# A four-layer network with expert layers on one core: expert slots in a room per expert, layer 3's routing during its attention, second biases inside the expert groups

## The chip, the cores and the metric

The kernel runs on one core of a Trainium2 chip. The core has a matrix engine (TensorE, PE in the profile; PEld is its loading of weights), a vector engine (VectorE, DVE), a scalar engine (ScalarE, ACT), a general engine (GpSimd, POOL) and a queue engine (SyncE, SP)[...] and 16 DMA engines. On-chip memory has 128 partitions; matrix products land in PSUM. The metric is the device time of one execution in microseconds. All figures below are the core's own.

## The reference

Input x is 32 sequences of 256 tokens with 128 channels (8192 tokens). Four layers follow, each x = x + attn(norm(x)) and then x = x + ffn(norm(x)), in float32. What matters here:

```
# layer 0 ffn: expert-choice experts and a shared expert
# layer 1 ffn: 8 experts, hidden 512, top 2 of 8 by x @ gate_w + gate_b
gw = softmax(top_w)
out = sum_e combine[:, e] * (gelu(x @ w1[e] + b1[e]) @ w2[e] + b2[e])
shared = gelu(x @ ws1 + bs1) @ ws2 + bs2
# layer 3 ffn, on its normed input x:
x = layernorm(x + mha(x, 16 heads), ln1_g, ln1_b)
gp = softmax(x @ w_group + b_group)        # 4 groups, the best is taken
ep = softmax(x @ w_expert + b_expert)      # 2 experts in it, the best is taken
y_e = relu(x @ w1[e] + b1[e]) @ w2[e] + b2[e]   # hidden 256
x = layernorm(x + g_prob * e_prob * y_e, ln2_g, ln2_b)
```

The layer-3 result is added to that layer's input. The biases b2 and the norms' gains and shifts are not zero or one in the inputs.

## The kernel before

x stays on chip as 64 tiles of 128 tokens (K.x, named x_sb in the profile). Eight stage functions run one after the other: l0_attn, l0_ffn, l1_attn, l1_ffn, l2_attn, l2_ffn, l3_attn, l3_ffn. A scheduler orders instructions on each engine, except where manual_schedule says that an engine keeps the written order (the expert groups and the attention, on PE, ACT and DVE). Memory of a finished pool is given to the next tiles; the first instruction that writes the new tile then waits for the last use of the old.

*Expert slots (class Slots).* In layers 1 and 3 each token's row of 130 numbers (128 channels, the row number where its result goes, its weight) is sent to a table in the chip's main memory, sorted by expert. fill writes blank rows early in the kernel (POOL, 56 DMAs for both tables, behind layer 0's attention). places works out every token's slot: products with triangular and all-ones matrices count how many earlier tokens chose the same expert, a scan over tiles sums them, each expert's rows are rounded up to groups of 256, and so an expert's first slot is known only once all tokens are routed. send_all writes the tokens with indirect DMAs from POOL, one per tile and rank (line 382; 128 in layer 1, 64 in layer 3). experts then takes groups of 256 rows: DVE copies the group's expert weights (w, line 418, from w_all at an offset read from group_of), SP loads the rows (xs, line 420), PE transposes them, multiplies twice (hp line 436, o line 452) with ACT's activation between, DVE scales by the weight (y, line 457) and POOL scatters the result with two indirect DMAs (f_back, line 388). Fetch, rise and fall of three neighbouring groups overlap. There are 72 groups in layer 1 and 40 in layer 3; blank rows fill the rest. join loads the results in order and adds them.

*Layer 1 ffn.* Norm, gate (lp, line 1309), choice of two experts (beat, top), places, sends. While POOL sends, PE works the shared expert in 16 blocks of 512 tokens (lines 1346 to 1359), and the second biases, combine times b2, in 16 further blocks (lines 1363 to 1372, through the PSUM tiles hp and o that the shared expert uses).

*Layer 3 ffn.* attention (line 1389) is also used by layer 2. It goes through 32 batches (one sequence each) in steps: PAIRS = 8 steps t to a batch, and in each step a written mixture of scores for a later batch (s and top), weights and values for the present one (t, e, o), and in certain of the eight places p = t % 8 the projection of a batch ahead and the output of the one before (heads, back, join). rows(b) makes the normed input of a batch on POOL (line 1893). Its PSUM tile m (pool pm) is shared by projections and outputs. Before the first batch its tiles val, k and q are cleared on POOL (lines 1417 to 1423). After attention come the first norm (DVE, line 121, then gain and shift on POOL, lines 1936 and 1937), transposes and gate (ge, line 1966), softmax and argmax over groups and experts, places, 64 sends, bias blocks (line 2003), experts, join, and the second norm with the last addition. The weights w_all are loaded in a burst on SP just after attention (lines 1922 and 1923). build then stores the result in eight DMAs.

## Time and profile before

| | us |
|---|---|
| three runs | 3464.90, 3453.68, 3464.75 (median 3464.75) |
| the profiled execution | 3465.69 |
| its span | 3463.6 |
| mean granted clock of PE | 0.874 |
| PE busy | 2774.8 (80%) |
| DVE busy | 1871.7 (54%) |
| ACT busy | 1331.2 (38%) |
| POOL busy | 801.7 (23%) |

The stages, as read from the trace (us from the span's start): l0_attn to 367, l0_ffn to 874, l1_attn to 1014, l1_ffn to 1631 (norm and routing to 1108, sends to 1277, bias blocks to 1320, experts to 1598, join), l2_attn to 2261, l2_ffn to 2393, l3_attn to 2490, l3_ffn to the end (attention to 3070, first norm and routing to 3158, sends to 3241, experts to 3369, join to 3386, second norm and stores).

In the views, a time is that of one profiled execution. "idle before <-releaser" says how long an engine stood before an instruction and what ended the wait. A busy PE is not PE at its peak, and a DMA-issuing instruction is not counted as busy. Groups are named by line of the kernel, engine, operation and the program's tile names.

### The profile page before, as it was taken

The numbers are of one execution on the slowest core, as the hardware profiler recorded it, in microseconds if no ns is written. First come the engines' busy times: TensorE is split into PE (matmuls) and PEld (weight loads), VectorE is DVE, ScalarE is ACT, GpSimd is POOL, SyncE is SP. The second block draws the span as 40 slices with busy tenths as digits, with TensorE's granted clock in tenths as the row PEclk, the third lists the DMA queues.
The fourth block names the chain that finished last, engine by engine and source line by source line (L and its number), as shares of the span: only waits on it lengthen the run. The fifth ranks groups of instructions, "written<-read, shape, count | busy, mean of one in ns | idle before, by whom it ended". The sixth has DMA issues, their size and how long they took to land.

```text
span 3463.6 us, 57988 instructions
## 1 busy us (share of the span) xinstructions
PE 2774.8 (80%) x22018; PEld 1924.6 (56%) x22018; DVE 1871.7 (54%) x4141; ACT 1331.2 (38%) x2801; POOL 801.7 (23%) x1009
## 2 busy tenths in 40 slices
PE   5999787999979829994699999967888888975660
PEld 4765444448557518993466666656455555554550
DVE  6115345337674003445666666555677777774338
ACT  3323432224623303441155555611256666631120
POOL 0001420000232753554200000002140000035664
PEclk9899799999987958997599999958889999975695
DMA  2386420010010111224344444200144444410232
GB/s 64 122 256 202 131 69 1 29 31 3 2 55 9 51 46 46 72 71 127 98 125 125 125 125 125 77 3 6 35 139 124 125 125 128 121 29 27 69 101 74
DMA packets 252694, 285.05 MB, mean 82 GB/s; under 512 B 31971, under 2 KB 228192, under 8 KB 244224
## 3 DMA queue, kind: packets, MB, share of 16 engines
q1 hardware_dynamic: 213632, 228.32, 22.9%
q0 software_dynamic: 17984, 42.53, 3.8%
q10 hardware_dynamic: 20800, 10.49, 1.2%
q8 instruction: 175, 2.87, 0.3%
q14 instruction: 103, 0.84, 0.1%
HBM read 156.69 MB, written 122.45 MB: 81 GB/s over the span
## 4 chain that ended last, share of the span: by engine, by line
PE 55%; DVE 14%; POOL 6%; issue 5%; DMA 5%; ACT 4%; SPq 0%; POOLq 0%; ACTq 0%; DVEq 0%
PE t L1595 7%; PE o L1615 6%; PE hp L436 4%; PE o L452 4%; POOL f_rows L382 3%; PE s L1540 3%; PE m L1627 2%; DVE top L1553 2%; PE m L1500 2%; DMA f_rows<-row,slot 2%; POOL f_back L388 2%; DVE y L121 2%; PE o L1144 2%; ACT e L1603 2%; PE g L1105 2%
## 5 line engine op out<-in xcount | busy, mean ns | idle before, releaser
L1553 DVE TENSOR_REDUCE top<-s 128x6 f32<-128x768 f32 (+1 forms) x512 | 556.2, 1089 | 255.7 <-PE t L1476 88.9
L1603 ACT ACTIVATE e<-t 128x384 f32<-128x384 f32 (+1 forms) x1024 | 508.9, 546 | 177.8 <-PE t L1476 104.9
L1595 PE MATMUL t<-q,k 64*128 64x256 f32 (+1 forms) x2048 | 420.0, 306 | 38.1 <-ACT e L1603 37.1
L1540 PE MATMUL s<-k,q 48*128 48x256 f32 (+1 forms) x2048 | 421.0, 329 | 4.4 <-DVE top L1553 3.7
L1595 PEld LDWEIGHTS t<-q,k 64*128 64x128 f32 x2048 | 293.7, 189 | 155.9 <-ACT e L1603 91.8
L1615 PE MATMUL o<-e,val 128*32 128x256 f32 (+1 forms) x4096 | 303.1, 368 | 0.1
L1540 PEld LDWEIGHTS s<-k,q 48*128 48x128 f32 x2048 | 293.5, 196 | 11.5 <-DVE top L1553 8.0
L388 POOL DMA_INDIRECT f_back<-y,place x224 | 219.4, 980 | 184.6 <-DVE y L457 138.4
L442 ACT ACTIVATE h<-hp,w 128x256 f32<-128x256 f32 x368 | 154.3, 470 | 254.7 <-PE hp L436 249.1
L436 PE MATMUL hp<-xT,w 128*128 128x256 f32 x736 | 186.5, 393 | 24.4 <-DVE xT L427 24.3
L452 PE MATMUL o<-w,h 128*128 128x128 f32 x1472 | 184.8, 277 | 0.0
L452 PEld LDWEIGHTS o<-w,h 128*128 128x128 f32 x1472 | 175.6, 194 | 0.1
L1735 POOL TENSOR_SCALAR xn<-x_sb,mean_a,r_a 128x128 f32<-128x128 f32 x64 | 58.9, 929 | 459.6 <-PE m L1489 446.7
L436 PEld LDWEIGHTS hp<-xT,w 128*128 128x128 f32 x736 | 134.6, 195 | 44.4 <-DVE xT L427 30.0
L1476 PE MATMUL s<-hideq,pick 64*128 64x128 bf16 x1024 | 146.1, 230 | 0.0
L1476 PE MATMUL t<-hidek,pick 64*128 64x128 bf16 x1024 | 145.8, 225 | 0.0
L418 DVE COPY w<-w_all 128x1028 f32 (+1 forms) x112 | 67.5, 602 | 131.4 <-DMA f_rows<-row,slot 90.5
L128 PE MATMUL t<-ident,xn 128*128 128x128 f32 x320 | 72.0, 353 | 79.7 <-DVE xn L121 63.7
L382 POOL DMA_INDIRECT f_rows<-row,slot x128 | 122.8, 959 | 40.4 <-issue 29.9
L689 PE MATMUL up<-wc,hT 128*128 128x128 f32 x768 | 131.8, 313 | 0.0
L1494 POOL TENSOR_TENSOR y<-y,bias 128x256 f32<-128x256 f32 x32 | 22.0, 688 | 441.7 <-PE m L1489 441.7
L1615 PEld LDWEIGHTS o<-e,val 128*32 128x32 f32 x4096 | 81.2, 108 | 63.3 <-ACT out L1621 5.9
(522 smaller groups left out, 5493.8 us busy)
## 6 DMA issues: line engine op xcount, KB each, us to landing
d<-half SPq DMA_DIRECT2D x256, 256.0 KB
tz<-kpad SPq DMA_DIRECT2D x64, 512.0 KB
q<-d SPq DMA_DIRECT2D x128, 256.0 KB
k<-d SPq DMA_DIRECT2D x128, 256.0 KB
f_rows<-blank POOLq DMA_DIRECT2D x56, 260.0 KB, 3.2
xs<-f_rows SPq DMA_DIRECT2D x112, 130.0 KB
y_d<-ys SPq DMA_DIRECT2D x32, 256.0 KB
yt<-y_d SPq DMA_DIRECT2D x32, 256.0 KB
```

Of the source, the lines that this page charges most:

```text
L382: i = self.K.nc.gpsimd.indirect_dma_start(self.rows, bass.IndirectOffsetOnAxis(ap=slot[:, j : j + 1], axis=0), row, None)
L388: i = self.K.nc.gpsimd.indirect_dma_start(self.back, bass.IndirectOffsetOnAxis(ap=place, axis=0), row, None)
L436: nc.tensor.matmul(hp[:, i, :], w[:, (c + i) * P : (c + i + 1) * P], xT, start=True, stop=True,)
L442: nc.scalar.activation(h[:, c + i, :], hp[:, i, :], act, bias=w[:, b1 : b1 + 1])
L452: nc.tensor.matmul(o[:, i, :], h[:, c, i * P : (i + 1) * P], w[:, F + c * D : F + c * D + D], start=c == 0, stop=c == FC - 1,)
L689: nc.tensor.matmul(o, hT[:, 2 * blk + b, s : s + P], wc[:, j, cs], start=j == 0, stop=False)
L1476: nc.tensor.matmul(t.rearrange("p (n q) -> p n q", n=3)[:, 0:3:2, 64 * n : 64 * n + 64], pick[r, n, :], hide[name][r], start=False, stop=n ...
L1540: nc.tensor.matmul(s[:, j, lo:hi], q[r, p, h * P : (h + 1) * P], k[r, p, 0 : hi - lo], start=h == 0, stop=not causal and h == 1,)
L1553: nc.vector.tensor_reduce(tops[b][:, :, :, p].rearrange("q h j -> q j h"), out_of["s"][:, :, 0:used].rearrange("q j (h k) -> q j h k", h=n ...
L1595: nc.tensor.matmul(t[:, kh * SEQ : kh * SEQ + SEQ - late], k[r, p, kh * P : (kh + 1) * P], q[r, p, late:SEQ], start=kh == 0, stop=not caus ...
L1603: nc.scalar.activation(e, t, AF.Exp)
L1615: nc.tensor.matmul(o[32 * i : 32 * i + 32, late:SEQ], val[b % RING][:, kh, 4 * g + i, :], exps[4 * g + i][:, kh * SEQ : kh * SEQ + SEQ - l ...
```

## The change

1. The table of slots gets a fixed room for each of the 8 experts, 8448 rows each, so a slot no longer depends on the other experts' totals. The tables grow from 18432 and 10240 rows to 67584 each, and fill writes them in DMAs of 6 rows per partition that lie together in memory (176 DMAs instead of 56).
2. places is a generator that takes a chunk of tiles and carries the counts on in seen. finish computes from the totals which expert a group belongs to and at which row it starts; experts reads the start into a register of SP for its load. SP joins the engines in written order there.
3. In layer 3, the first norm, the routing and the sends run as steps (route) of attention's loop, for the chunks of tiles 0-16, 16-32, 32-48, 48-56 and 56-64, each once its tiles are complete: two steps in each attention step, and a step that needs PE only in two places of eight. What is left over runs after the last attention step. The norm is applied by ACT, gain and shift by POOL. Argmax over the groups is taken first and only the two experts of the best group are compared. The second norm's shift is added to x on POOL during attention. The tiles of begin, the norm's parameters and gate weights are taken ahead of attention; w_all is loaded in a pool opened after it.
4. The second biases are split into three bf16 parts and added inside each group by a product of depth 3 with a row of ones; the 16 bias blocks of each of the two layers are gone. In layer 1's shared expert one product per block adds its bias, and the output products accumulate onto it. w is 128 columns wider, of which three rows hold the parts.
5. The end goes in quarters of 16 tiles: results loaded on SP and added, statistics, norm on ACT, gain and addition on DVE, a store per four tiles. Layer 1's join loads on SP alone.

```diff
+    def second_biases(self, pool, dst, name):
+
+        nc = self.nc
+        n = dst.shape[1]
+        src = self.ins[name].rearrange("n d -> (n d)").unsqueeze(0)
+        t = pool.tile([3, n * D], F32, name="rows3")
+        nc.sync.dma_start(t, src.partition_broadcast(3))
+        rows = self.split(pool, t, self.parts(pool, 3), name)
+        nc.vector.tensor_copy(dst, rows.rearrange("p (n d) -> p n d", n=n))
...
     def close(self, lo, hi):
+        for _ in self.steps(lo, hi):
+            pass
+
+    def steps(self, lo, hi):
...
         nc.vector.tensor_add(mean, st[:, :, 1], st[:, :, 4])
+        yield
...
+    ROOM = NT * P + GROUP
...
-        self.count = self.groups * self.GROUP
+        self.count = self.NE * self.ROOM
...
-        n = 4
+        n = 6
...
-        rows = self.rows.rearrange("(t p) w -> p t w", p=P)
+        rows = self.rows.rearrange("(c p n) w -> c p n w", p=P, n=n)
...
+            nc.gpsimd.dma_start(rows[i], t)
...
+    def begin(self, pool, most):
+
+        nc = self.K.nc
+        self.every = pool.tile([P, P], BF16, name="every")
+        self.first = pool.tile([P, P], BF16, name="first")
+        nc.gpsimd.memset(self.every, 1.0)
...
+        self.go_on = pool.tile([P, self.NE, most], F32, name="go_on")
+        nc.gpsimd.memset(self.go_on, 1.0)
+        nc.gpsimd.memset(self.go_on[:, :, 0:1], 0.0)
+        self.seen = pool.tile([P, self.NE], F32, name="seen")
+        self.floor = pool.tile([P, self.NE], F32, name="floor")
+        for t in (self.seen, self.floor):
+            nc.gpsimd.iota(
+                t, pattern=[[self.ROOM, self.NE]], base=0, channel_multiplier=0,
+                allow_small_or_imprecise_dtypes=True,
+            )
...
+    def places(self, pool, bank, picks, out):
+
+
+        NE = self.NE
...
+        t = bank()
...
+        yield "PE"
+        nc.tensor.matmul(before, self.first, taken, start=True, stop=True)
+        nc.tensor.matmul(total, self.every, taken, start=True, stop=True)
...
+        slot = new("slot").rearrange("p (e n) -> p e n", e=NE)
+        nc.vector.tensor_sub(slot, sums, total)
+        nc.vector.tensor_add(slot, slot, before)
+        yield
+        nc.vector.tensor_add(slot, slot, self.seen.unsqueeze(2).to_broadcast([P, NE, n]))
+        nc.vector.tensor_add(self.seen, self.seen, sums[:, :, n - 1])
+        yield
+        for m, u in zip(picks, out):
+            mine = new("mine").rearrange("p (n e) -> p n e", e=NE)
+            s = pool.tile([P, most], F32, name="place")[:, 0:n]
+            nc.vector.tensor_mul(mine, m, slot.rearrange("p e n -> p n e"))
+            yield
...
+    def finish(self, pool, long, expert, start):
...
+                at = nc.sync.value_load(
+                    start[0:1, g : g + 1], min_val=0, max_val=self.count - self.GROUP
+                )
+                xs = gp.tile([P, N, self.WIDE], F32, name="xs")
+                nc.sync.dma_start(
+                    xs, self.rows[bass.ds(at, self.GROUP)].rearrange("(n p) w -> p n w", p=P)
+                )
                 at = nc.vector.value_load(
-                    group_of[0:1, g : g + 1], min_val=0, max_val=(self.NE - 1) * LONG
+                    expert[0:1, g : g + 1], min_val=0, max_val=(self.NE - 1) * LONG
                 )
...
+                b2 = gp.tile([3, D], BF16, name="b2")
+                nc.scalar.copy(b2, w[0:3, 2 * F + FC :])
...
+                    nc.tensor.matmul(o[:, i, :], self.every[0:3, :], b2, start=False, stop=True)
...
-                engines={nc.tensor.engine, nc.scalar.engine, nc.vector.engine}
+                engines={nc.tensor.engine, nc.scalar.engine, nc.vector.engine, nc.sync.engine}
...
+        nc.gpsimd.memset(w_all[:, :, 2 * F + FC :], 0.0)
...
+        S.begin(sp, NT)
...
+                K.second_biases(K.pool(bs, "f1b", 1), w_all[0:3, :, 2 * F + FC :], "f1_b2")
...
+            S.finish(cp, LONG, expert, start)
+            for n in range(2):
+                S.belongs(row, 0, NT, n)
+                nc.gpsimd.tensor_copy(row[:, :, D + 1], weight[:, n, :])
+                for j in range(NT):
+                    S.send(slots[n][:, j : j + 1], row[:, j, :])
...
+                nc.tensor.matmul(
+                    o, S.every[0:3, :], b2.unsqueeze(1).to_broadcast([3, 4, D]), start=True,
+                    stop=False,
+                )
...
-            for blk in range(NBLK):
-                t = ph.tile([NE + 1, 512], F32, name="hp")
-                for i in range(4):
-                    nc.tensor.transpose(t[:, i * P : (i + 1) * P], cmb[:, 4 * blk + i, :], K.ident)
-                cmbT = hw.tile([NE + 1, 512], F32, name="cmbT")
-                nc.scalar.copy(cmbT, t)
-                o = po.tile([P, 4, D], F32, name="o")
-                for i in range(4):
-                    nc.tensor.matmul(
-                        o[:, i, :], cmbT[:, i * P : (i + 1) * P], b2, start=True, stop=True
-                    )
-                xb = K.x[:, 4 * blk : 4 * blk + 4, :]
-                nc.vector.tensor_add(xb, xb, o)
             cs.close()
 
...
+        if more:
+            more(t, bank)
+
+    def bank():
+        return pm.tile([P, 512], F32, name="m")
...
-        for t in range(-LEAD, total + PAIRS):
+        for t in range(-LEAD, total + PAIRS + (PAIRS if more else 0)):
...
+        S.begin(sp, 16)
+        ln = K.load_bcast(sp, "f3_ln", 4 * D).rearrange("p (n d) -> p n d", n=4)
...
+                K.second_biases(K.pool(bs, "f3b2", 1), b2, "f3_b2")
...
+            def route(bank, lo, hi):
+
+
+                n = hi - lo
+                for _ in after.steps(lo, hi):
+                    yield
...
+                for k in range(lo, hi, 4):
+                    four = y[:, k : k + 4, :]
+                    for j in range(k, k + 4):
+                        nc.scalar.activation(
+                            y[:, j, :], y[:, j, :], AF.Identity, bias=nmr[:, j : j + 1],
+                            scale=after.r[:, j : j + 1],
+                        )
+                        yield
+                    nc.gpsimd.tensor_mul(four, four, spread(4, 0))
+                    nc.gpsimd.tensor_add(four, four, spread(4, 1))
+                for k in range(lo, hi, 4):
+                    yield "PE"
+                    t = bank()
+                    K.transpose4(t, y[:, k : k + 4, :])
+                    yT = rw.tile([P, 512], F32, name="yT")
+                    nc.scalar.copy(yT, t)
+                    yield "PE"
+                    t = bank()[:, 0 : 4 * (NG + NE)].rearrange("p (n e) -> p n e", n=4)
+                    for i in range(4):
+                        nc.tensor.matmul(
+                            t[:, i, :], yT[:, i * P : (i + 1) * P], gate_w, start=True, stop=True
+                        )
+                    nc.vector.tensor_add(
+                        lge[:, k - lo : k - lo + 4, :], t,
+                        gate_b.unsqueeze(1).to_broadcast([P, 4, NG + NE]),
+                    )
+                yield
...
+                yield from S.places(rw, bank, [pick.rearrange("p n g e -> p n (g e)")], [slot])
+                for j in range(lo, hi):
+                    S.send(slot[:, j - lo : j - lo + 1], row[:, j, :])
+            work, held = [], [None]
+            cuts = [16, 32, 48, 56, 64]
+            def more(t, bank):
+                if t is None:
+                    while work:
+                        if next(work[0], work) is work:
+                            work.pop(0)
+                    return
+                b, p = t // PAIRS - 2, t % PAIRS
+                if p == 0 and 0 <= b < NB:
+                    after.take(y, 2 * b, 2 * b + 2)
+                    two = K.x[:, 2 * b : 2 * b + 2, :]
+                    nc.gpsimd.tensor_add(two, two, spread(2, 3))
+                    if 2 * b + 2 in cuts:
+                        i = cuts.index(2 * b + 2)
+                        work.append(route(bank, cuts[i - 1] if i else 0, cuts[i]))
+                for _ in range(2):
+                    if work:
+                        if held[0] == "PE" and p not in (1, 2):
+                            return
+                        held[0] = next(work[0], work)
+                        if held[0] is work:
+                            held[0] = None
+                            work.pop(0)
+                        if held[0] == "PE":
+                            return
+            attention(K, ps, "f3", rows, wq, wk, wv, qb, kb, wo, bias, y, False, more)
...
+            w_all = K.pool(ps, "f3wa", 1).tile([P, NE, LONG], F32, name="w_all")
...
+            nc.gpsimd.memset(w_all[:, :, 2 * F + FC :], 0.0)
+            nc.scalar.copy(w_all[0:3, :, 2 * F + FC :], b2)
+            S.finish(K.pool(ps, "f3n", 1), LONG, expert, start)
+            S.experts(w_all, expert, start, F, AF.Relu)
...
+            ps.enter_context(K.tc.manual_schedule(engines={nc.scalar.engine, nc.vector.engine}))
+            bp = K.pool(ps, "f3b", 4)
+            last = first
+            def join(i):
+                t = S.results(bp, 0, i)
+                nc.vector.tensor_add(y[:, i : i + 8, :], y[:, i : i + 8, :], t)
+                last.take(y, i, i + 8)
+            def close(lo, hi):
+                last.close(lo, hi)
+                nc.vector.scalar_tensor_tensor(
+                    nmr[:, lo:hi], last.mean[:, lo:hi], -1.0, last.r[:, lo:hi], ALU.mult, ALU.mult
+                )
+                for j in range(lo, hi):
+                    nc.scalar.activation(
+                        y[:, j, :], y[:, j, :], AF.Identity, bias=nmr[:, j : j + 1],
+                        scale=last.r[:, j : j + 1],
...
-        S.join(y)
...
+            def end(i):
+                s = slice(i, i + 4)
+                nc.vector.tensor_mul(y[:, s, :], y[:, s, :], spread(4, 2))
+                nc.vector.tensor_add(K.x[:, s, :], K.x[:, s, :], y[:, s, :])
+                nc.sync.dma_start(dst[:, s, :], K.x[:, s, :])
+            for q in range(5):
+                if q < 4:
+                    for i in (16 * q, 16 * q + 8):
+                        join(i)
+                    close(16 * q, 16 * q + 16)
+                if q:
+                    for i in range(16 * q - 16, 16 * q, 4):
+                        end(i)
```

## The prediction

> **What bounds the kernel now.** I read the busy time of each engine by stage first (columns: window, its length, then busy time of PE, PEld, DVE, ACT and POOL with instructions, granted clock, DMA share, GB/s).
>
> ```profile
> 1108.00:1278.00 170.00, 86.87 (x504) 63.14 (x503) 12.84 (x23) 33.34 (x49) 127.18 (x164) 0.77 0.15 51
> 1278.00:1320.00 42.00, 39.65 (x173) 32.14 (x174) 12.46 (x20) 8.04 (x14) 2.49 (x8) 0.50 0.05 13
> 1320.00:1598.00 278.00, 273.01 (x1881) 253.19 (x1880) 117.48 (x288) 120.78 (x288) 139.03 (x144) 0.98 0.24 68
> ...
> 2480.00:3070.00 590.00, 516.15 (x4963) 297.94 (x4961) 413.99 (x667) 370.66 (x771) 74.99 (x120) 0.95 0.41 117
> 3070.00:3158.00 88.00, 55.98 (x228) 44.91 (x229) 77.69 (x177) 12.56 (x25) 41.47 (x50) 0.50 0.10 28
> 3158.00:3241.00 83.00, 41.55 (x164) 29.16 (x162) 10.81 (x17) 8.02 (x14) 61.41 (x64) 0.50 0.16 52
> 3241.00:3368.00 127.00, 94.07 (x560) 80.39 (x560) 53.12 (x161) 33.53 (x80) 80.39 (x80) 0.92 0.30 84
> 3368.00:3386.00 18.00, 0.00 (x0) 0.00 (x0) 9.23 (x9) 0.00 (x0) 0.00 (x0) 0.50 0.95 233
> 3386.00:3463.00 77.00, 0.00 (x0) 0.00 (x0) 70.39 (x162) 0.00 (x0) 41.38 (x32) 0.50 0.19 55
> ```
>
> Layer 1's sends are POOL's (128 x 1.26 us), 42 us of bias blocks follow, and its experts are PE's (273 of 278). Layer 3's attention is PE's (516 of 590) with DVE behind it; then norm and routing (88), sends (83), experts, join (18) and second norm (77) stand in a row, most of it on one engine each.
>
> Why bias blocks are not under the sends shows in who waited for the sent rows, and in the timeline where the sends end:
>
> ```profile
>   DVE w L418: 90.5, 1
> ```
>
> ```profile
> 1274.65 0.96 POOL L382 DMA_INDIRECT f_rows<-row,slot  x1 [0.30 <-DMA f_rows<-row,slot]
> 1277.61 0.70 DVE L418 COPY w<-w_all 128x1028 f32 x1 [90.47 <-DMA f_rows<-row,slot]
> 1279.52 0.68 DVE L1359 TENSOR_TENSOR x_sb<-x_sb,o 128x512 f32<-128x512 f32 x1
> 1280.35 2.04 PE L1368 MATMUL o<-w_f_b,cmbT 9*128 9x128 f32 x8 [85.27 <-DVE x_sb L1359]
> ```
>
> The first expert's weight copy (its tile w) stands on DVE ahead of most bias additions and waits for all sends; PE stands 85 us behind that.
>
> Third, POOL's timeline as layer 3's second half starts: the clears of val, k and q run during layer 3's first half, the first rows at 2495.15.
>
> ```profile
> 2393.41 1.84 POOL L1417 MEMSET val<- 128x1024 f32 x2
> ...
> 2409.39 1.88 POOL L1423 MEMSET q<- 128x2048 f32 x1
> 2489.42 1.31 POOL L491 IOTA y<- 128x4 f32 x16 [78.15 <-PE o L1868]
> 2495.15 6.99 POOL L1893 TENSOR_SCALAR y<-x_sb,mean_f,r_f 128x128 f32<-128x128 f32 x9 [4.41 <-DVE r_f L259]
> ```
>
> Last, one expert group of layer 1 in the timeline, whose period is 3.73 (next o at 1447.18), and PE's waits in steady attention (us in total, times, longest):
>
> ```profile
> 1442.54 0.70 DVE L418 COPY w<-w_all 128x1028 f32 x1 [0.41 <-DVE y L457]
> 1443.45 1.95 PE L452 MATMUL o<-w,h 128*128 128x128 f32 x16
> ```
>
> ```profile
> PEld t L1595 <- ACT e L1603: 53.9, 124, 1.3
> PE t L1595 <- ACT e L1603: 22.7, 27, 0.8
> ```
>
> PE has short gaps there, set by ACT's exponentials, none over 1.3 us: work put between is paid unless it falls into one of them.
>
> [...] The trace shows 2.3 us for a sent 64 KB row block and 3.2 us for a 260 KB fill[...]. [...] 0.50 in 3070 to 3241, 0.92 in the experts. The routing left in the tail is priced at half clock.
>
> **The change part by part** (us; sum against the profiled 3465.7, span 3463.6 plus 2.1; the median is 0.9 below it).
>
> *Fill.* 56 DMAs of 260 KB become 176 of 400 KB. The old ones take 1.97 each (367.1 to 475.2), two buffers, so half of issue, iota and landing (0.77+0.13+3.2). [...] Layer 0's second half, busy on PE until 874 (203 of 258, then 164 of 165), covers it; POOL is next needed around 874-920. Cost 0; without cover 12.
>
> *Layer 1, bias blocks gone.* The last send lands 1277.2, xs takes 2.2, a transpose and DVE's copy under 1: first hp at about 1281 instead of 1321. -41 (bounds -35, -42). The shared blocks get one more matmul each, under the sends. Splitting the biases and the reordered place arithmetic are a dozen small DVE operations (0.2 to 1.2 each) against removed ones: -1, bounds -3, +4.
>
> *Layer 1's experts.* PE-bound at 3.73 a group (16 o matmuls in 1.95, so 0.12 each). Two more of depth 3 per group: +0.22x72=+16. From below 0 (no PE slot lost); from above 0.23 each as the row of bf16 pick matmuls has it: +33. The wider weight copy (0.70 to 0.79) and ACT's bias copy fall into idle time (DVE 117, ACT 121 of 278); SP's register read is new and unpriced by the trace; xs has four buffers, so up to some 7 us of it is hidden by the groups before, and behind it on SP stands only the next xs.
>
> *Layer 3 start.* begin()'s memset `every` now takes memory that layer 3's first half uses to its end (2489); behind it on POOL stand begin()'s iotas, the val clear, which in the compiled order also waits for the last DVE operation of the bias split (8 on 3x1024, with the norm's closing operations between them: to about 2500), then the 18 us of clears, and behind those rows(0), for which PE, then all of attention, waits. 2500+18=2518 instead of 2495: +22; without the split's wait +13.
>
> *Routing inside attention.* Steps stand in the written PE, ACT and DVE orders, two per attention step, those that need PE in two of eight places, with one shared PSUM bank. In the static DVE order chunks 0 to 2 (48 tiles) run within attention, and chunks 3 and 4 (8 tiles each) wholly after it. DVE gets two bn_stats a batch (0.28 each): of 16.7 per batch some 0.35 lengthens, x30=+10. A 16-tile chunk adds ACT 16x0.37=6, PE 16 transposes at 0.28 and 32 gate matmuls at about 0.12 with a bank round trip for every four tiles, DVE about 45 operations of 0.2. As PE already fills 87%, I count PE 11, ACT 3.5, DVE 3.5, closing 1 = 19 a chunk, for two chunks (the third overlaps the draining end): +38, less a little: sum with the statistics +46. POOL gets 48 tiles x 1.25 of scaling, 48 sends x 1.26 and 32 additions x 0.69 (the second norm's beta onto x): 143 us on an engine with 75 of 590 busy, so nothing, but a send waiting for its slots holds the rows and bias additions of the next batches behind it; these are issued a few batches ahead, which is the cover. From below +15 (all into ACT's and DVE's idle 200), from above +110 (every one of some 70 steps a chunk stalls PE 0.5).
>
> *Layer 3's tail.* From attention's end T0 (3070) to first hp (3245) it takes 175. After, in order on POOL: the 16 sends of chunk 2 to T0+17; chunk 3's scaling and shift, queued behind them (4 x 1.25) to +22; transposes and gate at half clock, one bank, 4.3 per four tiles, +30.5; softmax, argmax and places, some 30 small dependent operations, +38; 8 sends x 1.26, +48.5. Chunk 4's scaling is queued behind these sends: +53.5, gate +62, places +70, sends +80, landed +82. Only then may the weight load begin, as its memory holds routing tiles that the last send reads (in before it ran at 218 GB/s under the statistics): 2.1 MB, +94; clear, bias and weight copies, +98. 175-98: -77 (bounds -100, -45).
>
> *Layer 3's experts.* 2.95 a group, a loop of POOL's scatters and their landing; PE has a quarter free. +0.1x40=+4 (0, +12).
>
> *End.* Last result lands 3369; 94.6 to the end, in which DVE does join, statistics, and per 4 tiles the scaling. After, per quarter of 16 tiles: two joins 2.4, statistics 16x0.2, closing 3, gamma and addition 8x0.69: 14.1, x4=56, the ACT scaling in between; first load 4, last store 3: 63. Loads (8) and stores (16 of 256 KB instead of 8 of 512) share SP's queue; a store waiting for DVE holds only loads of the next quarter, of which four buffers are under way. -31 (bounds -45, -15).
>
> Sum: -41-1+16+22+46-77+4-31 = -62, so 3404.
>
> **Rivals.** (a) *Routing steps break attention's pace*: its orders are written by hand and in order, so a PE item waiting for its bank or a POOL scaling holds the batch's own matmuls. For it: PE is at 87%, and ACT and DVE feed each other at 1 us grain. Against it: only two PE places a batch. At +65 above my +46 the gain is gone; a stall of 4.5 per batch x30=+135 gives 3493, slower. (b) *Routing sinks into idle time*: DVE has 176 and ACT 219 idle in 590. Attention +10 to +20, 3370. (c) *The tail is slower than worked*: chunks 3 and 4 wait for POOL alternately, the weight load and register-addressed loads of the experts cost more: tail -45, experts +12 and +33, about 3460, same. (d) *The fill isn't hidden*, above 2.9 us each: +12, inside the first case.
>
> **How the numbers follow.** Forecast case 0.60 (own range 3375 to 3438), (b) 0.14 (3345 to 3385), (c) 0.11 (3438 to 3475), (a) 0.15 (3475 to 3530). 0.5%, about what can be told from no change, is 17 us: 3447 to 3482. Faster 0.60+0.14+a fifth of (c) = 0.76; same the rest of (c) and a little of (a), 0.11; slower 0.13. From 3348 to 3472 leaves out some 0.2.
>
> **What would show it.** Layer 1's first expert hp 3 to 5 us after the last send lands; group period near 3.95; rows(0) of layer 3 near 2517; attention near 18 per batch while chunks run; sends on POOL inside it; after it two send bursts of 8, then a burst of weight DMAs before the first hp, PE idle; a last stage near 63. Wrong if attention grows by over 100, if the group period is above 4.2, or if experts start later than 130 after attention.

## The result and the profile after

The changed kernel takes 3478.55 us (median of 19 runs, 3458.63 to 3493.28), the kernel before 3460.86 beside it (19 runs, 3449.95 to 3468.86). The ratio is 1.0054, 95% interval 1.0039 to 1.0069: slower by half a per cent, where 3404 was forecast. The profiled span is 3474.8 against 3463.6. It grew by 11.2; the medians differ by 17.7.

Busy times by stage of the changed kernel (columns as in the same view of before: window, its length, then PE, PEld, DVE, ACT, POOL with instructions, granted clock, DMA share, GB/s):

```profile
1108.00:1282.00 174.00, 94.38 (x526) 64.85 (x524) 18.75 (x38) 33.86 (x50) 125.53 (x138) 0.78 0.16 51
1282.00:1610.00 328.00, 323.09 (x2021) 276.49 (x2020) 122.35 (x289) 130.38 (x359) 142.49 (x144) 0.99 0.21 59
...
2590.00:3100.00 510.00, 439.28 (x3975) 255.24 (x3968) 347.01 (x656) 313.08 (x665) 74.71 (x80) 0.90 0.39 112
3100.00:3192.00 92.00, 82.18 (x704) 47.92 (x703) 48.22 (x113) 52.98 (x109) 6.16 (x7) 0.85 0.14 39
3192.00:3280.00 88.00, 13.70 (x55) 11.04 (x56) 22.67 (x129) 10.93 (x26) 37.99 (x38) 0.50 0.18 53
3280.00:3406.00 126.00, 113.79 (x638) 90.09 (x636) 54.53 (x155) 40.17 (x119) 77.22 (x80) 0.93 0.28 80
3406.00:3475.00 69.00, 0.00 (x0) 0.00 (x0) 56.57 (x184) 25.06 (x64) 0.12 (x1) 0.50 0.44 123
```

The 42 us of bias blocks are gone (experts begin at 1282), but layer 1's experts fill 328 us where they filled 278. Attention shows a clock of 0.90 and 0.85 where it had 0.95 over a longer stretch that took in its slow beginning. Attention's end to layer 3's experts is one row of 88 us where two rows made 171, and the end is 69 instead of 77 after a join of 18.

Read from the two traces, stage by stage (us):

| | before | after | difference | forecast |
|---|---|---|---|---|
| span's start to layer 1's first expert hp | 1320.9 | 1282.6 | -38 | -42 |
| layer 1's first hp to layer 2's first statistics | 288.0 | 334.7 | +47 | +16 |
| from there to layer 3's last x before its second half | 881.1 | 870.0 | -11 | 0 |
| that x to the first rows of attention | 5.1 | 27.6 | +22 | +22 |
| first rows to attention's first output | 70.6 | 71.5 | +1 | 0 |
| attention, first to last output | 504.1 | 605.9 | +102 | +46 |
| attention's end to layer 3's first hp | 175.2 | 87.3 | -88 | -77 |
| layer 3's first hp to the span's end | 218.5 | 195.3 | -23 | -27 |
| sum | 3463.6 | 3474.8 | +11 | -62 |

Two rows are wrong: layer 1's experts and attention.

**Layer 1's experts.** The timeline of one group of the changed kernel (start, length, engine, line, operation):

```profile
1444.59 0.97 PEld L545 LDWEIGHTS o<-w,h 128*128 128x128 f32 x8
...
1445.68 0.09 PEld L549 LDWEIGHTS <-every 3*128 3x128 bf16 x1
1445.69 0.22 PE L549 MATMUL o<-b,every 3*128 3x128 bf16 x1
1445.84 0.97 PEld L545 LDWEIGHTS o<-w,h 128*128 128x128 f32 x8
...
1446.93 0.09 PEld L549 LDWEIGHTS <-every 3*128 3x128 bf16 x1
...
1447.09 1.59 PEld L529 LDWEIGHTS hp<-xT,w 128*128 128x128 f32 x8
```

The weight loads of the first four output products end at 1445.56. The load for the depth-3 bias product begins 0.12 later and takes 0.09, and the next large load begins at 1445.84, a further 0.07 on. From the start of one run of four products to the next is 1.25 with the bias product. The period of a group is 4.44, that of before 3.73: 0.71 more, 0.35 for each of two small products, times 72 groups 51 us.

**Attention.** The waits of PE between the first and last outputs (us in total, times, longest), first lines:

```profile
PE t L1675 <- ACT e L1683: 19.5, 25, 1.6
PE m L1569 <- DVE y L1732: 16.1, 27, 0.8
PE m L2061 <- DVE row L1659: 10.1, 11, 1.0
PE m L1607 <- ACT oT L1721: 9.6, 27, 0.4
PE m L138 <- DVE half L1589: 8.7, 9, 1.0
```

Only the third and fifth (the gate, line 2061, and the transposes of normed rows, line 138) are routing's. With the waits of routing's other steps, for the slots, they make 23.6 us, far from 102. What the waits do is in the clock. PE's timeline of one such place:

```profile
2774.55 0.63 PE L138 MATMUL m<-ident,y 128*128 128x128 f32 x4 [0.97 <-DVE half L1589]
...
2775.78 0.64 PE L1695 MATMUL o<-e,val 128*32 128x256 f32 x8
...
2777.83 1.06 PE L2061 MATMUL m<-w_f_gate_w,yT 128*128 128x12 f32 x8 [0.98 <-DVE row L1659]
2778.82 0.58 PE L1675 MATMUL t<-q,k 64*128 64x256 f32 x1
...
2779.97 1.08 PE L1695 MATMUL o<-e,val 128*32 128x256 f32 x8
```

and the same stretch in windows of 4 us:

```profile
2772.00:2776.00 4.00, 3.03 (x34) 1.80 (x36) 2.58 (x7) 3.07 (x7) 0.00 (x0) 1.00 0.56 187
2776.00:2780.00 4.00, 2.96 (x30) 2.05 (x22) 1.95 (x6) 1.10 (x3) 0.00 (x0) 0.85 1.05 282
2780.00:2784.00 4.00, 4.00 (x30) 2.02 (x28) 2.45 (x4) 1.88 (x4) 0.00 (x0) 0.50 0.24 68
2784.00:2788.00 4.00, 3.65 (x25) 2.24 (x21) 1.08 (x2) 1.58 (x5) 0.00 (x0) 0.50 0.00 0
```

PE waits a microsecond for the transposes and another for the gate, is busy for three quarters of two windows, and then the clock is 0.50 for about 10 us: the eight value products, 0.64 at 2775.78, take 1.08 at 2779.97. The records of the granted clock show 17 such episodes before attention's draining end, each 3.4 us or a multiple of it. With 7 us at the end itself they make 133.5 us between the first and last output; before, there were 3.8 us, all at the end.

### The profile page after: what moved, and what is told of

The parts are those of the page before. It is cut to its first block, busy times and chain, and to the rows that moved or that the text cites. A ratio compares the mean times of both kernels' runs of the same rounds, so it can differ in the third digit from the quotient of the medians.

```text
span 3474.8 us, 58674 instructions
## 1 busy us (share of the span) xinstructions
PE 2796.0 (80%) x21876; PEld 1904.0 (55%) x21878; DVE 1836.1 (53%) x4293; ACT 1379.9 (40%) x3014; POOL 845.1 (24%) x1166
## 4 chain that ended last, share of the span: by engine, by line
PE 42%; DVE 12%; POOL 7%; issue 5%; ACT 3%; DMA 2%; SPq 0%; POOLq 0%; DVEq 0%; ACTq 0%
PE t L1675 7%; PE o L1695 6%; POOL f_rows L470 4%; PE o L545 4%; PE hp L529 4%; DVE top L1633 3%; PE s L1620 3%; PE m L1707 2%; POOL f_back L476 2%; PE m L1580 2%; PE m L1607 1%; ACT e L1683 1%; PE s L1556 1%; PE t L1556 1%; PE lp L1386 1%
## 5 line engine op out<-in xcount | busy, mean ns | idle before, releaser
L1675 PE MATMUL t<-q,k 64*128 64x256 f32 (+1 forms) x2048 | 433.2, 315 | 34.1 <-ACT e L1683 33.7
L1620 PE MATMUL s<-k,q 48*128 48x256 f32 (+1 forms) x2048 | 435.0, 338 | 3.8 <-DVE top L1633 3.7
L1675 PEld LDWEIGHTS t<-q,k 64*128 64x128 f32 x2048 | 304.6, 197 | 148.6 <-ACT e L1683 78.5
L1695 PE MATMUL o<-e,val 128*32 128x256 f32 (+1 forms) x4096 | 317.0, 383 | 0.0
L1620 PEld LDWEIGHTS s<-k,q 48*128 48x128 f32 x2048 | 305.7, 204 | 10.9 <-DVE top L1633 8.0
L545 PE MATMUL o<-w,h 128*128 128x128 f32 x1472 | 214.8, 285 | 0.0
L545 PEld LDWEIGHTS o<-w,h 128*128 128x128 f32 x1472 | 183.8, 193 | 7.8
L511 DVE COPY w<-w_all 128x1156 f32 (+1 forms) x112 | 74.9, 669 | 150.3 <-POOL late L1540 84.4
L551 DVE TENSOR_TENSOR y<-o,xs 128x256 f32<-128x256 f32 x112 | 47.6, 425 | 163.7 <-PE o L549 163.7
L518 PE MATMUL t<-ident,xs 128*128 128x128 f32 x224 | 44.6, 282 | 106.7 <-DMA xs<-f_rows 106.7
```

The lines of the kernel that those rows point to most:

```text
L545: nc.tensor.matmul(o[:, i, :], h[:, c, i * P : (i + 1) * P], w[:, F + c * D : F + c * D + D], start=c == 0, stop=False,)
L1620: nc.tensor.matmul(s[:, j, lo:hi], q[r, p, h * P : (h + 1) * P], k[r, p, 0 : hi - lo], start=h == 0, stop=not causal and h == 1,)
L1675: nc.tensor.matmul(t[:, kh * SEQ : kh * SEQ + SEQ - late], k[r, p, kh * P : (kh + 1) * P], q[r, p, late:SEQ], start=kh == 0, stop=not caus ...
L1695: nc.tensor.matmul(o[32 * i : 32 * i + 32, late:SEQ], val[b % RING][:, kh, 4 * g + i, :], exps[4 * g + i][:, kh * SEQ : kh * SEQ + SEQ - l ...
```

## The experiments

Each is a small edit of the changed kernel and was timed beside the kernel before. The ratios are to that kernel; the changed kernel's own was 1.0054. Stage times are read from one profiled execution of each.

### Layer 1's experts: is it the product, its data type, or its depth?

**The products left out.** The second biases of both layers' experts are then missing.

```diff
-  w[...], start=c == 0, stop=False,
+  w[...], start=c == 0, stop=c == FC - 1,
   )
-nc.tensor.matmul(o[:, i, :], self.every[0:3, :], b2, start=False, stop=True)
```

> Leaves the products of the second biases out of the expert groups of both layers (the narrow copies and the wider weight copy stay), so the experts' second biases are not added. Theory M: the two depth-3 products in each group are the whole lengthening of layer 1's expert period from 3.73 to 4.44 us: the period falls back to 3.7 to 3.8, its experts take 50 us less than in the changed kernel, the time falls to about 3428. Rival W: the wider weight copy, ACT's copy of the biases or the register-addressed load set the period: it stays above 4.3 and the time above 3465.

3430.09 us, ratio 0.9909 (0.9884 to 0.9935). The period is 3.73 again, to the digit that of before. So the wider weight copy, ACT's cast of the bias and SP's register read lengthen the period by nothing, and all of the 0.71 is the two products. The ratio fell by 0.0145, 50 us, where 0.71x72 is 51.

**The products in float32**, straight from w with a float32 row of ones.

```diff
-nc.tensor.matmul(o[:, i, :], self.every[0:3, :], b2, start=False, stop=True)
+nc.tensor.matmul(o[:, i, :], K.three, w[0:3, 2 * F + FC :], start=False, stop=True)
```

> The two products per group stay, but in float32 from the weight tile itself, with a row of ones in float32; ACT's copy to bf16 goes. Theory S: what costs is the change of PE between float32 and bf16 products, 0.35 us per product: the period of layer 1's groups falls to about 3.97 (two products at the 0.12 of the other output products), time about 3445. Rival D: what costs is the shallow product (3 rows), or any product between the others: the period stays within 0.1 of 4.44 and the time within 8 of the changed kernel's.

3533.79 us, ratio 1.0221 (1.0176 to 1.0265). The period is 4.95. The timeline of this kernel's group:

```profile
1439.81 0.97 PEld L546 LDWEIGHTS o<-w,h 128*128 128x128 f32 x8
...
1440.90 0.29 PEld L550 LDWEIGHTS o<-w,three 3*128 3x128 f32 x2
1440.91 0.48 PE L550 MATMUL o<-w,three 3*128 3x128 f32 x2
1441.32 0.97 PEld L546 LDWEIGHTS o<-w,h 128*128 128x128 f32 x8
```

There is no change of type left, and the holes are still there: the large load ends at 1440.78, the small one begins 0.12 later, ends at 1441.19, and the next large one begins 0.13 after that. The product itself is now two records, as each float32 output product is, and so dearer: neither forecast had that. A change of data type is not needed for the holes.

**One product a group**, ahead of the output products and over both halves at once.

```diff
+nc.tensor.matmul(
+    o, self.every[0:3, :], b2.unsqueeze(1).to_broadcast([3, N, D]), start=True, stop=False,
+)
 for i in range(N):
     for c in range(FC):
-        ... start=c == 0, stop=False,
+        ... start=False, stop=i == N - 1 and c == FC - 1,
-    nc.tensor.matmul(o[:, i, :], self.every[0:3, :], b2, start=False, stop=True)
```

> One bf16 product of depth 3 for both token tiles of a group, put before the output products, instead of two. Theory S (each change of type costs): one product less, period about 4.09, layer 1's experts 25 us shorter, time about 3452. Rival: the cost is that the product waits for ACT's copy of the biases: then placed earlier it waits more, and the period does not fall.

3458.23 us, ratio 0.9992 (0.9977 to 1.0007). The period is 4.14: 0.41 above that without products, where two products cost 0.71. The cost goes nearly by the number of products: this one writes 256 columns, each of the two 128. It falls although the product stands earlier, so it is not a wait for ACT's copy.

**The same two products over all 128 rows**, with zeros below the three.

```diff
-b2 = gp.tile([3, D], BF16, name="b2")
-nc.scalar.copy(b2, w[0:3, 2 * F + FC :])
+b2 = gp.tile([P, D], BF16, name="b2")
+nc.scalar.copy(b2, w[:, 2 * F + FC :])
-nc.tensor.matmul(o[:, i, :], self.every[0:3, :], b2, start=False, stop=True)
+nc.tensor.matmul(o[:, i, :], self.every, b2, start=False, stop=True)
```

> The two bf16 products per group take all 128 rows (ones times the biases' three rows and 125 rows of zeros) instead of 3; nothing else changes. Theory D: what costs 0.2 us on top of each product is the change between a product over 128 rows and one over 3 rows[...]: without it the period of layer 1's groups falls from 4.44 to about 4.0 and the time to about 3447. Rival S: it is the change between float32 and bf16: the period stays at 4.4. The float32 run, where each product cost 0.61 with the same gap ahead of it, speaks for D.

3446.34 us, ratio 0.9946 (0.9926 to 0.9965). PE's timeline of this kernel:

```profile
1443.07 1.06 PE L545 MATMUL o<-w,h 128*128 128x128 f32 x8
1443.96 0.22 PE L549 MATMUL o<-b,every 128*128 128x128 bf16 x1
1444.02 1.11 PE L545 MATMUL o<-w,h 128*128 128x128 f32 x8
```

The next output products begin 0.06 after the bias product begins, where 0.15 lay between in the changed kernel's timeline. The period is 3.95, and (3.95-3.73)/2 = 0.11 for each product instead of 0.35. A product of 3 rows among products of 128 rows costs 0.24 more here than the same product padded with zeros to 128, with identical type, count and place. What is shown is the effect of the row count; a change of data type alone, which these products of 128 rows still bring, costs at most the 0.11. Why PE holds its loads back around the product of 3 rows, no run here shows.

### Attention: is it the work, the waits, or the clock?

**All routing after attention.**

```diff
-for _ in range(2):
+for _ in range(0):
     if work:
         if held[0] == "PE" and p not in (1, 2):
```

> The routing steps are not taken during attention but all after it; statistics and the additions of the second norm's shift stay in attention. Theory R: the steps' work and the half clock that they bring are what lengthened attention from 575 to 677 us: attention falls to about 585 with a granted clock of 0.99 or more in its steady part; the tail grows by the three chunks, 150 to 190, and the time is about 3560. Rival P: statistics and POOL's additions lengthen attention: it stays above 640, with clock dips.

3529.21 us, ratio 1.0212 (1.0189 to 1.0235). Attention takes 520.5 with 16.8 at half clock, and the tail 220.2. (The tail grew by 133 where 150 to 190 had been expected.) The window view of 2700 to 2800, this kernel's line first, that of the changed kernel in the second fence:

```profile
2700.00:2800.00 100.00, 88.07 (x880) 50.57 (x872) 73.66 (x121) 64.82 (x136) 3.44 (x5) 0.98 0.43 123
```

```profile
2700.00:2800.00 100.00, 86.70 (x776) 50.20 (x768) 66.43 (x126) 63.80 (x138) 12.91 (x13) 0.88 0.37 104
```

PE is busy as long in both, but at 0.98 of the clock it passes 880 records and at 0.88 only 776: a busy PE is no measure of progress. Taking half of the half-clock time off, attention is 502 before, 512 in this kernel and 539 in the changed one. So the norm's statistics and shift additions cost 10 us, the routing steps 27, and the lower clock (133.5-3.8)/2 = 65. These three make the 102.

That half a microsecond is lost for each at half clock can be read from kernels whose attention is that of the changed kernel: itself, the four with edits in the expert groups, and the two below on layer 3's start and on the weights. Their profiles have 108 to 144 us of half clock in attention, which takes 594.1 to 609.8. A straight line through the seven gives 0.46 us for each at half clock, and with half of it taken off all seven lie between 537.6 and 540.1. So half clock varies by up to 36 us, and attention by up to 16, without any edit there; only larger differences count in what follows.

**The places of PE's steps moved apart**, from 1 and 2 to 1 and 6 of eight.

```diff
-if held[0] == "PE" and p not in (1, 2):
+if held[0] == "PE" and p not in (1, 6):
```

> The routing steps that need PE are taken in places 1 and 6 of a batch's eight instead of 1 and 2; same work. Theory C: transposes and gate a step apart, each with a wait of 1 us for the shared bank, leave PE too idle[...]; in attention 126 us of half clock in the changed kernel. Apart, half clock falls below 40 us, attention shortens by 40 to 50 and the time is about 3435. Rival N: the narrow gate products (12 columns) bring it, wherever they stand: half clock stays above 90 us and the time within 10.

3453.75 us, ratio 0.9983 (0.9963 to 1.0002). Attention takes 576.9, of which 83.4 at half clock. The edit adds and removes no work. Attention fell by 29.0 and half-clock time by 50.1, 0.58 for each. Both forecasts were missed: half clock fell, but not below 40.

**The gate padded to 128 columns**, zeros in the 116 added.

```diff
-gate_w = K.load(wp, "f3_gate_w")
+gate_w = wp.tile([P, P], F32, name="gate_w")
+nc.gpsimd.memset(gate_w, 0.0)
+nc.sync.dma_start(gate_w[:, 0 : NG + NE], ins["f3_gate_w"])
-t = bank()[:, 0 : 4 * (NG + NE)].rearrange("p (n e) -> p n e", n=4)
+t = bank().rearrange("p (n e) -> p n e", n=4)
-lge[:, k - lo : k - lo + 4, :], t,
+lge[:, k - lo : k - lo + 4, :], t[:, :, 0 : NG + NE],
```

> The gate products of layer 3's routing are padded from 12 to 128 columns (zeros), so that PE works at full width while they run; places stay 1 and 2. Rival N (narrow products bring the half clock): half clock in attention falls from 126 us below 40, and the time to about 3440 although each quad of tiles costs 0.4 us more. Theory C (the two waits so near each other): half clock stays above 90 us, the time within 10 of the changed kernel's or some us above.

3453.3 us, ratio 0.9974 (0.9962 to 0.9985). Attention takes 578.3, of which 57.2 at half clock. Its waits, lines of the same view as above, then its first gate products and the windows of 4 us around them:

```profile
PE m L2063 <- DVE row L1659: 10.1, 11, 1.0
PE m L138 <- DVE half L1589: 8.7, 9, 1.0
```

```profile
2780.63 1.16 PE L2063 MATMUL m<-gate_w,yT 128*128 128x128 f32 x8 [0.98 <-DVE row L1659]
```

```profile
2776.00:2780.00 4.00, 2.62 (x30) 1.24 (x22) 3.42 (x9) 3.40 (x7) 0.00 (x0) 1.00 0.94 293
2780.00:2784.00 4.00, 3.37 (x34) 2.54 (x36) 2.22 (x6) 1.09 (x2) 0.00 (x0) 1.00 0.95 236
```

The waits are those of the changed kernel to the tenth, PE has more to do than there, and the kernel is quicker. So it isn't the waits' own length that costs most. Here too PE waits twice for a microsecond, and the clock stays at 1.00. That tells the clock from every account in which routing's work or its waits hold the batches back. With half of the half-clock time off, attention is 549.7, 10 more than in the changed kernel: the padding costs that much, and wins 38 through the clock. Rival N's forecast, below 40 us, was missed too: not all half clock comes from the gate.

**Both.**

> Both at once: gate products padded to 128 columns and PE steps in places 1 and 6. Each alone took attention from 606 us (first to last output) to 577 and 578, with half clock down from 134 us to 83 and 57. [...] they add: half clock below 30 us, attention about 555, time about 3440. If they are two ways to the same end, or the rest comes from the waits for the bank, half clock stays at 50 or more and the time at 3453.

3446.46 us, ratio 0.9954 (0.9937 to 0.997). Attention takes 569.3, and 51.7 at half clock remained where under 30 had been expected. The two edits overlap.

The episodes of half clock in the changed kernel's attention last 3.4, 6.8, 10.2 or 13.7 us, and in the clock records they begin and end on one grid with a step of 3.41. With PE's records the share of busy time in each step of that grid (a window, below) can be worked out. In the changed kernel's attention 138 windows were at full clock. Eighteen of them were followed by half clock, and none of these was idle: PE was busy for 0.35 to 0.70 of 17 of them, and 0.79 of one. Of the 120 followed by full clock the lowest were 0.66, 0.71 and 0.72. Of the 17 half-clock windows followed by full, the lowest had 0.99. In the kernel before, no window but two at the draining end was under 0.75. With places 1 and 6 the falls came at up to 0.74 to 0.76, so the share alone doesn't tell which windows are followed by half clock.

What the share leaves out shows in the windows in which the 12 sets of gate products of attention begin (us; the third column is the half clock that follows them at once):

| | sets followed by half clock | half clock after them | half clock in attention |
|---|---|---|---|
| changed kernel | 9 of 12 | 72 | 133.5 |
| places 1 and 6 | 8 of 12 | 41 | 83.4 |
| gate padded | 0 of 12 | 0 | 57.2 |
| both | 0 of 12 | 0 | 51.7 |

The first eight windows of the changed kernel are busy for 0.70, and half clock follows each. In the padded kernel seven are busy for 0.70 or 0.71, and full clock follows. So at the same share the narrow products lose the clock and the padded ones keep it, as rival N had it for these places: eight of 12 columns take 1.06 us in the records, eight of 128 take 1.16, and the records don't tell them apart. The 72 us are nearly all of what padding saves (76), and moving the places shortens the episodes rather than avoiding them. This is why the two edits don't add. Of the eight falls that remain in the last kernel five come as a chunk starts, where PE waits for ACT's exponentials (up to 1.6 us in the waits of the changed and the padded kernel), and one at the products that count the slots. What would remove these wasn't tried.

### Layer 3's start

**The clears ahead.** The slots' begin only takes its tiles ahead of attention (begin_tiles); its constants are filled (begin_fill) from more, at t == 0, so behind the clears of val, k and q. A gap tile moves the memory of the bias split off val; one more small tile of the biases moves to another pool.

```diff
-S.begin(sp, 16)
+S.begin_tiles(sp, 16)
...
+def begin():
+    S.begin_fill()
     S.belongs(row, 0, NT, 0)
+K.pool(bs, "f3gap", 1).tile([P, 23 * 1024], F32, name="gap")
 K.second_biases(K.pool(bs, "f3b2", 1), b2, "f3_b2")
```

> Layer 3's clears of val, k and q stand ahead of begin's memset on POOL again, and the memory of the bias split no longer lies under val; the iotas of begin come after them. If the step of the prediction is right, the first rows of layer 3's second half start 20 us earlier against the end of its first half, all the rest is as in the changed kernel, and the time is about 3459. If something else held the first rows, less than 8.

3463.3 us, ratio 1.0002 (0.9985 to 1.002). POOL's timeline, of the changed kernel and then of this one:

```profile
2496.94 1.86 POOL L1497 MEMSET val<- 128x1024 f32 x2 [9.04 <-DVE b L115]
...
2513.07 1.80 POOL L1503 MEMSET q<- 128x2048 f32 x1
2514.86 6.99 POOL L1994 TENSOR_SCALAR y<-x_sb,mean_x,r_x 128x128 f32<-128x128 f32 x9
```

```profile
2409.49 1.84 POOL L1506 MEMSET val<- 128x1024 f32 x2
...
2425.55 1.92 POOL L1512 MEMSET q<- 128x2048 f32 x1
...
2512.03 6.99 POOL L2002 TENSOR_SCALAR y<-x_sb,mean_x,r_x 128x128 f32<-128x128 f32 x9 [5.39 <-DVE r_x L292]
```

In the changed kernel the clear of val waits for the last copy of the bias split (b, line 115), then 18 us of clears stand ahead of the rows. With the clears early the rows come 6.0 after the last x instead of 27.6. Of these 21.6 us some 5 are given back: the first half of layer 3 takes 96.1 with the clears in it, as it took 96.2 before, and 91.1 in the changed kernel. The ratio moved by 0.0052, 18 us.

### Weights earlier in the tail

**The weight load ahead of the last sends.** The weights are put where attention's tiles were, by a gap tile, instead of on routing's.

```diff
+K.pool(ps, "f3gap2", 1).tile([P, 5 * 1024], F32, name="gap2")
 w_all = K.pool(ps, "f3wa", 1).tile([P, NE, LONG], F32, name="w_all")
```

> The weights of layer 3's experts are loaded into memory that attention has left instead of memory that the last routing steps still use, so that the load can start at attention's end, behind the last sends. The prediction's step: the load of 2.1 MB stands alone on the path, 12 us after the last send. The tail from attention's end to the first expert product falls from 87 to about 76, the time to about 3467. Rival: the groups' rows, the bias copies and the group table hold the first product anyway: under 4 us.

3467.65 us, ratio 1.002 (1.0005 to 1.0035). PE's timeline at the end of the tail, of the changed kernel and then of this one:

```profile
3210.45 1.11 PE L138 MATMUL m<-ident,y 128*128 128x128 f32 x4 [18.77 <-POOL y L2051]
...
3237.63 1.12 PE L138 MATMUL m<-ident,y 128*128 128x128 f32 x4 [15.12 <-POOL y L2051]
...
3276.79 0.69 PE L518 MATMUL t<-ident,xs 128*128 128x128 f32 x2 [27.09 <-DMA xs<-f_rows]
3279.49 2.07 PE L529 MATMUL hp<-xT,w 128*128 128x256 f32 x4 [2.02 <-DVE xT L520]
```

```profile
3267.04 0.69 PE L518 MATMUL t<-ident,xs 128*128 128x128 f32 x2 [16.53 <-DMA xs<-f_rows]
3268.25 2.08 PE L529 MATMUL hp<-xT,w 128*128 128x256 f32 x4 [0.52 <-DVE xT L520]
```

The tail goes from 87.3 to 76.0, and the ratio moved by 0.0034, 12 us. The first fence also shows the rest of it: chunks 3 and 4 wait for POOL's scaling in turn (18.77 and 15.12), each behind the sends of the chunk before.

### All together

One product a group over 128 rows, the padded gate, places 1 and 6, early clears and early weights.

> All that the runs point to together: one bias product per group over 128 rows, gate products of 128 columns in places 1 and 6, clears ahead of begin's memset, and the weights' load at attention's end. If the gains add, against the changed kernel: layer 1's period 4.44 to 3.87 (41), attention 40, layer 3's start 16, tail 11, together about 105: 3370, 2.6% under the kernel before. If they overlap or the clock gives part back, 3400.

3369.6 us (5 runs, 3358.63 to 3370.52), ratio 0.9733 (0.9706 to 0.9761): it beats both kernels, by 92 us the one before. Its windows:

```profile
1274.00:1555.00 281.00, 280.14 (x1940) 259.49 (x1939) 126.45 (x290) 131.52 (x359) 142.10 (x142) 0.99 0.24 67
...
2560.00:3091.00 531.00, 460.73 (x4382) 268.54 (x4380) 368.01 (x729) 343.36 (x726) 78.79 (x84) 0.95 0.39 109
3091.00:3169.00 78.00, 14.70 (x56) 11.17 (x57) 22.44 (x127) 10.93 (x26) 38.13 (x38) 0.50 0.14 39
```

Layer 1's experts are back at 281, period 3.84 (one product at 0.11). Attention is at 568.3 with 51.2 of half clock, the tail at 76.9. The group and the attention edits repair the two rows of the table that went wrong, and what was forecast for the bias blocks and the tail is then kept. The forecast for this kernel, 3370, was the sum of the single gains.

## Why the prediction was wrong, point by point

- *Fill.* Right. 176 DMAs of 390 KB went out from 363.5 to 677.9, 1.79 each, under layer 0's second half, and cost nothing. At the 2.9 each of rival (d), an estimate that lets the 3.2 of a 260 KB landing grow with the size, they would have taken 510 us in all; they took 314. (The 390 count 1024 bytes, the prediction's 400 a thousand.) Issue fell from 0.77 to 0.56 and landing from 3.2 to 2.8 us, although each carries more; the rows of a DMA now lie together, but no run parts that from the size.
- *Layer 1, bias blocks gone.* Right: -38 for -42.
- *Layer 1's experts.* **This step failed.** It priced each product at 0.12, from 16 records in 1.95, and forecast a period of 3.95. Two faults lie in it. The 16 records are eight float32 products of two records each. That one did no harm, as a bf16 product is one record: padded to 128 rows the products cost 0.11 and the period was 3.95, as forecast. The other is that the step took the depth for free, "two more of depth 3". At 3 rows among 128 each costs 0.35. The term is +51 by periods (+47 by stage) instead of +16. Its upper bound of 0.23 each, +33, was too low as well, because it was read from bf16 products that stand among their like. The trace of before has no product of few rows between others of 128 in the experts, but it has one in layer 0's attention, a bias of 12 rows:

```profile
130.72 0.74 PEld L689 LDWEIGHTS up<-wc,hT 128*128 128x128 f32 x6
131.59 0.09 PEld L692 LDWEIGHTS <-inside 12*128 12x128 bf16 x1
131.75 0.74 PEld L689 LDWEIGHTS up<-wc,hT 128*128 128x128 f32 x6
```

The holes are the same, 0.13 and 0.07. From one run of six loads to the next is 1.03, where six loads that follow each other every 0.11 take 0.67: about 0.36 for the product. The price could have been read there.

- *Layer 3 start.* Right, mechanism and size: the wait for the split and 18 us of clears, +22. It missed that the first half of layer 3 gets 5 us quicker without the clears. The kernel before and the two kernels here with the clears in that stage have 96.1 to 96.3, the ten without 90.9 to 92.5; why the clears slow it wasn't tried. The remaining 6 of the -11 in the table lie between layer 1's end and layer 3's start, in stages that no edit touches. The part from layer 2's first statistics to its first output is 130 to 131 in seven of the thirteen profiles, the changed kernel among them, and 137 to 140 in six, that of before among them; no edit sorts them.
- *Routing inside attention.* **This step failed too.** It counted work on PE, ACT and DVE: +46. The work and its waits came to +37, statistics 10 and routing 27, so the count was fair. What it left out was the clock of PE, for attention left as it was at 0.95: +65 more. More than half of that half clock follows the gate's products of 12 columns, which it priced by their time alone. The prediction priced half clock in the tail only. PE at "87%" was not a stage with 13% to spare: its weakest windows, 0.75 busy, kept the clock, and with a wait of 1 us and narrow products in them, 0.70 busy in eight, they lost it.
- *Layer 3's tail.* Right: -88 for -77, in the worked order: two send bursts of 8, then the weights after the last send, then hp. Each step was a little quicker than worked: chunk 3's sends end at T0+43 (48.5 forecast), chunk 4's at +70 (80), the weights are issued to +81 (94).
- *Layer 3's experts and end.* Right. The last result lands 128 us after the first hp instead of 124, +4 as forecast; from there to the end it takes 67.4 instead of 94.6, -27 for -31.

Of the rivals, (a) came nearest: attention grew by 102, between the forecast and (a)'s figure. Its mechanism was not what happened. Steps waiting for a bank or for POOL hardly show in the waits (23.6 us, all for DVE). They had a larger effect by another way. That the time, 3479, lies in (a)'s range is luck: 31 of what was missed came from the experts' products, which (a) leaves as forecast. The prediction said that it would be wrong if attention grew by over 100 or a group's period passed 4.2; both happened (102 and 4.44). Either alone would have left the kernel faster: +11 less 31 (47-16) is -20, and less 56 (102-46) is -45.

## What to carry to other kernels

Before work is put into the gaps of a PE-bound loop, look at PE's waits, its narrow products and its share of busy time in windows of 3.4 us, not at the mean. In this loop, whose weakest windows stood at three quarters, a wait of 1 us beside products of 12 columns brought up to 14 us at half clock, of which about half was lost (0.46 by the line through seven kernels). Padding these products cost 10 us and won 38; spreading the steps won 29. Before a new product is priced, look for one like it, neighbours included, anywhere in the trace. The bias added here as a product of 3 rows between products of 128 rows was cheaper when padded with zeros to 128 (0.11 each instead of 0.35), and cheaper still as one product for both halves (0.11 a group instead of 0.22). When tiles of a later stage are taken early, look at whose memory they get: here both the clears ahead of the rows and the weights behind the last sends stood in line for memory, not for data.

## What the runs showed of the hardware that was not expected

- In layer 1's experts a bf16 product of 3 rows between products of 128 rows cost 0.24 us more than the same product padded to 128 rows (0.35 and 0.11); the float32 product of 3 rows has like holes in the weight loads around it (0.12 and 0.13, against 0.12 and 0.07).
- In the changed kernel's attention half clock came after 3.4 us windows in which PE was busy for 0.35 to 0.79, at most 0.70 in all but one, and full clock returned only after windows of 0.99 or more, though not after each; the episodes last up to 13.7 us. Seven kernels with this attention lose 0.46 us for each at half clock.
- Adding useless columns to the gate made the kernel faster: half clock fell from 133.5 to 57.2, attention by 27.6. At the same busy share of 0.70, windows with gate products of 12 columns lost the clock and those with 128 columns kept it.
